# Moving a few small operations at three seams of a fused graph and attention kernel: exponential tables, degrees, the last tile's statistics, and the output bias

## The chip, the cores and the metric

The kernel runs on one core of one Trainium2 chip, as a single program. A core has five engines, each with an instruction stream of its own that it works off in order: TensorE (PE; its weight loads are listed as PEld), VectorE (DVE), ScalarE (ACT), GpSimd (POOL) and SyncE (SP, which here issues all the DMAs). The metric is the device time of one execution in microseconds (us). Where a text here gives a point in time, it is counted from the first instruction of the profiled execution.

## The reference

A graph of 1250 nodes and 41250 edges (each edge in both directions, and a loop at every node), with 512 features per node, goes through four blocks. Each adds its result to `x`, and each starts from a layer normalisation of `x`:

```python
x = x + gnn0(layernorm(x))   # h@wc + (sum over neighbours of h@wn)/count + bias
x = x + ffn0(layernorm(x))   # layernorm; causal attention, 8 heads of 64, q and k l2-normalised;
                             # then 8 experts with gelu, weighted by a softmax gate
x = x + gnn1(layernorm(x))   # layernorm(h@W_self.T + mean_of_neighbours@W_neigh.T + bias)*gamma + beta
x = x + ffn1(layernorm(x))   # depthwise convolution of width 3 over the nodes, added to its input;
                             # qkv; attention over the 16 largest logits per query and head; @wo_w.T + wo_b
```

All of it is in float32. The degree by which `gnn1` divides is the number of edges that end in a node, at least 1.

## The kernel before

The 1250 nodes are cut into T = 10 tiles of P = 125. `X[125, 10, 512]` stays in SBUF through the whole kernel and takes each block's result. The 512 features are K = 4 slices of 128. Products in float32 alternate between a weight load and a matmul on TensorE. What has to be exact runs in a faster format as a high and a low part (the names `hi` and `lo`), with the same matmul done for both.

In nearly all of the kernel the order of instructions is written out by hand (`manual_schedule`); the framework only adds the semaphores. In the experts after the first one and in the first half of the second graph block, the framework's own scheduler chooses the order. What an engine is given later waits behind everything given to it before, also where that waits for another engine.

**Projections to the first attention.** For each tile, q, k and v are made (`project0`), squared and summed (`squares0`, L963 to L967), and the square root is taken on ScalarE (L1054 for q, L1059 for k). q is scaled (L972), turned and kept (`keep_q0`, L977); v is copied to `V` (L1065); k is turned and split into two parts by `keep_k0` (ScalarE L983, then VectorE L984, twice per tile). In the last tile the scores of the first step, `scores0(0, 0)` (TensorE L1034 and L1038), are issued ahead of v. After the loop come the maximum (`largest0`, VectorE L1091), the exponential (`weights0`, ScalarE L1101) and `keep_k0` of the last tile, then three VectorE operations on `deg`: a sum into `edges` (L1212), a maximum with 1 (L1213) and a reciprocal (L1214). `edges` is read at the very end of the kernel and `deg` in the second graph block (`joined1`, L1413).

The first attention has 40 steps (10 tiles by 4 pairs of heads), each for two heads. A step does the scores of the next step, the exponentials, the turns of the step before (`turns0`: TensorE L1122, copies by ScalarE L1127 or VectorE L1125) and the values of the one before that. The two heads' score buffers are one each in PSUM, so the next scores of a head wait until its exponentials have been read. `halves0` makes the split queries for three steps on (ScalarE L1004, GpSimd L1005, two DMAs each).

**Second graph block to the second attention.** In the second graph block each tile is summed over neighbours (L870), joined (L1413), normalised and scaled (L1421, L1422, then GpSimd L1423 and L1424, which writes `X`). The next block starts at once: `stats1` (L636 to L640) and `normed1` (L644) normalise a tile, `turn1_` turns it (TensorE L859, ScalarE L1439 to L1444), and `conv1` does the convolution for a range of tiles and some slices (ScalarE L1453, VectorE L1454 and L1455). `project1_` makes q or k of a range of tiles and some slices (TensorE L1462; q is kept by VectorE L1465, k by ScalarE L1471 and VectorE L1472 twice) and `values1_` makes v (TensorE L1477, VectorE L1483). The three buffers of `ps_mm` go round among all of these products. The output bias `wo_b` is added to `X` by VectorE: for tiles 0 to 7 behind a q or k product of the last tile range (L1530), for tiles 8 and 9 behind the last of them (L1532), and only then is `values1_(6, 7)` issued.

The second attention starts with two DMAs, the split queries of tile 0 (`halves1`: ScalarE L1580, GpSimd L1581, DMAs L1582 and L1583), and the first scores (`scores1`, L1595). Then 40 steps follow, each for two heads: a search for the 16 largest scores (VectorE L1602 to L1626), the exponentials (L1632), a sign that tells the chosen ones (L1639), their product (GpSimd L1642), turns (TensorE L1652, ScalarE L1659) and values (L1708). The values of the last three tiles are made during the first two steps (`values_late1`, `keep_late1` L1747).

ScalarE holds the tables of one set of functions at a time. Where an instruction needs another set, the compiler puts an `ACT_TABLE_LOAD` ahead of it, which the profile lists under that instruction's line.

Of the kernel before, what the change touches and what calls it, by code (L numbers as in the profile page):

```python
# [9 lines left out]
F32 = mybir.dt.float32  # L10
# [5 lines left out]
AF = mybir.ActivationFunctionType  # L16
ALU = mybir.AluOpType
AX = mybir.AxisListType

N = 1250  # L20
P = 125
T = N // P
# [550 lines left out]
def tile_usual(ctx: ExitStack, tc: tile.TileContext, a: dict, out: bass.AP):  # L573
    nc = tc.nc
# [11 lines left out]
    const_pool, const = pool("const", 1, "left")  # L586
# [38 lines left out]
    X = keep.tile([P, T, D], F32, name="X")  # L625
# [3 lines left out]
    deg = keep.tile([P, T], F32, name="deg")  # L629
    edges = keep.tile([P, 1], F32, name="edges")  # L630
# [59 lines left out]
    make_identity(nc, ident)  # L690
    ident16 = const.tile([128, 128], F16, name="ident16")
    nc.gpsimd.tensor_copy(ident16, ident)
    ones = const.tile([P, 1], F32, name="ones")
    nc.gpsimd.memset(ones, 1.0)

# [43 lines left out]
    with (  # L739
# [83 lines left out]
        for r in range(rounds):  # L823
# [7 lines left out]
            while order and (order[0][0] <= r or r == rounds - 1):  # L831
                _, i, t = order.pop(0)
# [10 lines left out]
    def ps_mm():  # L843
        return psum.tile([128, 512], F32, tag="mm", name="ps_mm")
# [28 lines left out]
    w_k = load_w(a["Wk"], "w_k")  # L873
# [82 lines left out]
    def project0(t, w):  # L956
        ps = ps_mm()
        product(ps[:P], hTs[t], 0, w)
        return ps
# [16 lines left out]
    def keep_q0(t, xn):  # L976
        nc.vector.tensor_scalar(qT[:, :, span(t, t + 1)], transposed(xn.rearrange("p h d -> p (h d)")),  # L977
                                qn_g, None, op0=ALU.mult)
# [65 lines left out]
    for t in range(T):  # L1044
        q = project0(t, w_q)
        if turned_k is not None:
            keep_k0(t - 1, turned_k)
        if t == T - 1:
            for n in range(3):
                halves0(n)  # L1050
        norm0(t + 2)
        q_ss = squares0(q)
        turn0(t + 1)
        nc.scalar.sqrt(q_ss, q_ss)  # L1054
        k = project0(t, w_k)
        qn = scaled0(q, q_ss)
        again0(t + 2)
        k_ss = squares0(k)
        nc.scalar.sqrt(k_ss, k_ss)  # L1059
        keep_q0(t, qn)  # L1060
        if t == T - 1:
            scores0(0, 0)
        v = project0(t, w_v)
        kn = scaled0(k, k_ss)
        nc.scalar.copy(V[:, t, :], v[:P])  # L1065
        turned_k = transposed(kn.rearrange("p h d -> p (h d)"))
        hTs.pop(t)
# [17 lines left out]
    with tc.tile_pool(name="att0", bufs=2, side="right", reuse_waits="tile") as at0:  # L1085
# [122 lines left out]
        weights0(0, 0)  # L1208
        keep_k0(T - 1, turned_k)


        nc.vector.tensor_reduce(edges, deg, AX.X, ALU.add)  # L1212
        nc.vector.tensor_scalar(deg, deg, 1.0, None, op0=ALU.max)  # L1213
        nc.vector.reciprocal(deg, deg)  # L1214
        psum_pool.__exit__(None, None, None)
        (ps_t0_pool, ps_t0), (ps_o0_pool, ps_o0), (ps_s0b_pool, ps_s0[1]) = (
            (p, p.__enter__()) for p in (tc.tile_pool(name=name, bufs=1, space=PSUM, reuse_waits="tile")
# [4 lines left out]
        for n in range(len(steps) + 2):  # L1222
            finish0()
            turns = turns0(n - 1)
            fills = fills0(n)

            def turn(last=False):
                for f in turns if last else turns[:1]:
                    f()
                del turns[: len(turns) if last else 1]  # L1230
                for f in fills if last else fills[:1]:
                    f()
                del fills[: len(fills) if last else 1]

            if n > 0:
                largest0(n, 0)
            turn()
            values0(n - 2, 0)
            for f in fills[:1] if n > 36 else ():
                fills.pop(0)()  # L1240
            if n > 0:
                weights0(n, 0)
            largest0(n, 1)
            if len(turns) > 2:
                turn()
            values0(n - 2, 1)
            scores0(n + 1, 0)
            weights0(n, 1)
            if len(turns) > 3:
                turn()  # L1250
            for f in fills[:1] if n > 36 else ():
                fills.pop(0)()
            values0(n - 2, 2)
            sums_over0(n)
            scale0(n - 2)
            if len(turns) > 1:
                turn()
            scores0(n + 1, 1)
            if len(turns) > 1:
                turn()  # L1260
            turn(last=True)
            halves0(n + 3)
            project0()
            if n == 2:
                nc.scalar.copy(b2_h, b2)
                nc.vector.tensor_sub(b2.bitcast(F32R), b2, b2_h.bitcast(F32))
                for i in (1, 3):
                    r = slice(i * E, (i + 1) * E)
                    nc.sync.dma_start(b2_h[r, :].bitcast(F32), b2[r, :])
            if n in (8, 16):  # L1270
                experts[n // 8 - 1] = load_expert(n // 8 - 1)
# [17 lines left out]
    wo_b = row(a["wo_b"], "wo_b", pool=rows1)  # L1289
# [98 lines left out]
    w_k, w_v = (wpool.tile([128, K, D], F32, tag="w", name=name) for name in ("w_k1", "w_v1"))  # L1388
# [59 lines left out]
    def conv1(t0, t1, *ks):  # L1448

        for k in ks:  # L1450
            c = xV[:, t0:t1, k * P : (k + 1) * P]
            at = hT[:, t0:t1, k, :]
            nc.scalar.activation(c, at[:, :, 1 : P + 1], AF.Identity, bias=pos_b[:, k : k + 1], scale=pos_m[:, k : k + 1])  # L1453
            nc.vector.scalar_tensor_tensor(c, at[:, :, :P], pos_w[:, k, 0:1], c, op0=ALU.mult, op1=ALU.add)  # L1454
            nc.vector.scalar_tensor_tensor(c, at[:, :, 2:], pos_w[:, k, 2:3], c, op0=ALU.mult, op1=ALU.add)  # L1455

    def project1_(t0, t1, w, *fs):
        n = (t1 - t0) * P
        for f in fs:
            ps = ps_mm()  # L1460
            for k in range(K):
                nc.tensor.matmul(ps[:, :n], w[:, k, f * 128 : (f + 1) * 128], xV[:, t0:t1, k * P : (k + 1) * P],  # L1462
                                 start=(k == 0), stop=(k == K - 1))
            if w is w_q:
                nc.vector.tensor_scalar(qT[:, f, span(t0, t1)], ps[:, :n], qk_b[:, f : f + 1],  # L1465
                                        float(D) ** -0.5, op0=ALU.add, op1=ALU.mult)
                continue
            for i, (own, other) in enumerate(PAIRS):
                hi, lo = (K2[r, 2 * f + i, span(t0, t1)] for r in (own, other))
                b = qk_b[own, K + f : K + f + 1]  # L1470
                nc.scalar.activation(hi, ps[own, :n], AF.Identity, bias=b)  # L1471
                nc.vector.scalar_tensor_tensor(lo, ps[own, :n], b, hi.bitcast(F32),  # L1472
                                               op0=ALU.add, op1=ALU.subtract)
# [36 lines left out]

    project1_(0, 2, w_q, 0, 1)
    turn1_(T - 2)
    conv1(2, 6, 2, 3)
    project1_(0, 2, w_q, 2, 3)
    stats1(T - 1)
    normed1(T - 1)
    project1_(0, 2, w_k, 0)
    turn1_(T - 1)
    project1_(0, 2, w_k, 1, 2, 3)
    values1_(0, 2)  # L1520
    for f in range(K):
        project1_(2, 6, w_q, f)
        conv1(6, 10, f)
    for f in range(K):
        project1_(2, 6, w_k, f)
    values1_(2, 6)
    for w in (w_q, w_k):
        for f in range(K):
            project1_(6, 10, w, f)
            nc.vector.tensor_add(X[:, f + 4 * (w is w_k), :], X[:, f + 4 * (w is w_k), :], wo_b)  # L1530
    for t in range(8, T):
        nc.vector.tensor_add(X[:, t, :], X[:, t, :], wo_b)  # L1532
    values1_(6, 7)
    manual.__exit__(None, None, None)
    close(slots_pool, work_pool, rows1_pool, gate_pool, stacks_pool, wpool_pool, rows_pool)
# [17 lines left out]
    with (  # L1553
# [17 lines left out]
        def halves1(i, a_):  # L1571
            if i >= T:
                return
            if a_ == 0:
                stacks[i] = at1.tile([128, 2, H, P], F32R, name="stacks")
            S = stacks[i]
            own, other = PAIRS[a_]
            hi, lo = S[own, 0, a_::2, :], S[own, 1, a_::2, :]
            q = qT[own, :, span(i, i + 1)]
            nc.scalar.copy(hi, q)  # L1580
            nc.gpsimd.tensor_sub(lo, q, hi.bitcast(F32))  # L1581
            nc.sync.dma_start(S[other, 1, a_::2, :].bitcast(F32), hi.bitcast(F32))  # L1582
            nc.sync.dma_start(S[other, 0, a_::2, :].bitcast(F32), lo.bitcast(F32))  # L1583

        def scores1(n, a_, *chunks):
            if n > last:
                return
            i, j = steps[n]
            h = 2 * j + a_
            if (n, a_) not in score:  # L1590
                score[n, a_] = ps_s1[a_].tile([P, 3 * 512], F32, name="S")
            for c in chunks:
                n0, n1 = PIECES[a_][c]
                for x in range(2):
                    nc.tensor.matmul(score[n, a_][:, n0:n1], stacks[i][:, x, h, :], K2[:, h, n0:n1],  # L1595
                                     start=(x == 0), stop=(x == 1))
# [168 lines left out]
        with tc.manual_schedule():  # L1765
            nc.sync.dma_start(w_v, a["qkv"][:, 2 * D :].rearrange("(k p) f -> p k f", p=128))
            nc.sync.dma_start(v_b, bass.AP(tensor=a["v_b"].tensor, offset=a["v_b"].offset, ap=[[0, P], [1, D]]))
            for a_ in range(2):
                halves1(0, a_)
            scores1(0, 0, 0, 2, 1)  # L1770
            for n in range(len(steps)):

# [63 lines left out]
            n, i = len(steps), T - 1  # L1836
# [103 lines left out]
```

## Time and profile before

| | |
|---|---|
| median of 3 runs | 1506.62 us (1504.06 to 1507.05) |
| the profiled execution | 1506.82 us |
| its span, first to last instruction | 1504.9 us |
| mean granted TensorE clock | 0.99 |
| busy: PE / DVE / ACT / POOL | 95% / 55% / 47% / 23% |
| table loads on ScalarE | 6, of 1.28 us each |
| PE idle for over 4 us | 3 times: 4.63 us before 322.04, 5.10 before 1021.02, 4.16 before 1110.07 |

The profile is of one execution. A busy share is an average over stages with different limits, so what a change is worth is read from the stretch in which it lies. In the timeline a row gives its start, its length, the engine, the line and the operation with its shapes; where the engine was idle before it, brackets give for how long and what ended that.

### The profile page before, as it was taken

How to read it: one execution, taken by the hardware profiler on the slowest of the kernel's cores; microseconds unless marked ns; L12 is line 12 of the kernel's file. 1: busy time of each engine (PE TensorE's matmuls, PEld its weight loads, DVE VectorE, ACT ScalarE, POOL GpSimd, SP SyncE). 2: the span in 40 equal slices, each digit the busy share in tenths (PEclk: the TensorE clock that was granted, in tenths of full speed). 3: DMA queues.
4: the chain of work that ended last, by engine and by line, in shares of the span. 5: the costliest groups of instructions: out<-in, count | busy, mean ns of one | idle time of the engine just before them, and what ended most of it. 6: DMA issues, size and time to landing. Idle time of an engine off the chain costs nothing. (4 is left out here: it accounts for less than half of the span.)

```text
span 1504.9 us, 22522 instructions
## 1 busy us (share of the span) xinstructions
PE 1424.8 (95%) x8127; PEld 936.5 (62%) x8127; DVE 830.4 (55%) x2852; ACT 707.8 (47%) x1351; POOL 350.1 (23%) x301
## 2 busy tenths in 40 slices
PE   6999999978999998999999999998988999999997
PEld 4566744457778776544544445664447788888885
DVE  8995667644444332341111263565377888887774
ACT  2334434455555553301111122432148999999984
POOL 0110000011111111000000021320026666666662
PEclk9999999989999999999999999999999999999999
DMA  4001000010101000201000000000020001001000
GB/s 141 30 0 57 1 0 1 1 47 16 43 15 49 21 24 18 63 28 56 29 28 28 28 29 29 0 29 0 5 79 15 15 22 25 22 23 25 22 9 24
DMA packets 42332, 41.19 MB, mean 27 GB/s; under 512 B 25738, under 2 KB 30084, under 8 KB 42211
## 3 DMA queue, kind: packets, MB, share of 16 engines
q1 hardware_dynamic: 42211, 39.66, 9.0%
q8 instruction: 66, 1.08, 0.3%
q14 instruction: 55, 0.45, 0.1%
HBM read 26.81 MB, written 2.56 MB: 20 GB/s over the span
## 5 line engine op out<-in xcount | busy, mean ns | idle before, releaser
L1642 POOL TENSOR_TENSOR e<-e,sg 125x1250 f32<-125x1250 f32 x79 | 203.5, 2575 | 127.0 <-ACT sg L1639 75.0
L1602 DVE MAX8 largest<-S 125x8 f32<-125x89 f32 (+1 forms) x1120 | 183.9, 241 | 51.3 <-PE S L1595 51.2
L1336 DVE SCALAR_TENSOR_TENSOR X<-ps_o,gate,X 125x512 f32<-125x512 f32 x80 | 60.0, 749 | 177.1 <-PE ps_o L1334 177.1
L1595 PE MATMUL S<-K,stacks 128*125 128x512 f32 x480 | 133.5, 389 | 14.3 <-ACT sg L1639 6.2
L1334 PE MATMUL ps_o<-we,hid 128*125 128x512 f32 x320 | 141.2, 595 | 0.0
L1659 ACT ACTIVATE pT<-ps_t 125x500 f32<-125x500 f32 x200 | 117.8, 589 | 37.7 <-PE ps_t L1652 32.7
L1652 PE MATMUL ps_t<-ident,e 125*125 125x125 f32 x800 | 132.2, 285 | 2.8 <-ACT pT L1659 1.3
L1652 PEld LDWEIGHTS ps_t<-ident,e 125*125 125x125 f32 x800 | 109.5, 187 | 35.1 <-ACT pT L1659 14.3
L1329 ACT ACTIVATE hid<-ps_mm,b 128x500 f32<-128x500 f32 (+1 forms) x40 | 24.6, 615 | 209.0 <-PE ps_mm L1326 209.0
L1326 PE MATMUL ps_mm<-yT,we 128*128 128x500 f32 (+1 forms) x320 | 115.8, 520 | 0.0
L1708 PE MATMUL O<-pT,yT 125*64 125x125 f32 x1600 | 104.7, 275 | 0.2 <-ACT pT L1659 0.2
L1632 ACT ACTIVATE e<-S,nm 125x1250 f32<-125x1250 f32 x80 | 104.4, 1305 | 0.2
L1639 ACT ACTIVATE sg<-S,below 125x1250 f16<-125x1250 f32 x80 | 104.5, 1307 | 0.0
L1334 PEld LDWEIGHTS ps_o<-we,hid 128*125 128x125 f32 x320 | 59.0, 187 | 72.4 <-issue 69.6
L1127 ACT COPY pT<-ps_t 125x500 f32<-125x500 f32 (+3 forms) x112 | 54.8, 489 | 94.3 <-PE ps_t L1122 93.3
L1326 PEld LDWEIGHTS ps_mm<-yT,we 128*128 128x128 f32 x320 | 60.3, 189 | 55.2 <-issue 53.3
L1595 PEld LDWEIGHTS S<-K,stacks 128*125 128x125 f32 x480 | 72.7, 190 | 33.8 <-ACT sg L1639 18.0
L1708 PEld LDWEIGHTS O<-pT,yT 125*64 125x64 f32 x1600 | 85.8, 136 | 10.5 <-DVE bad L1762 0.8
L1034 PE MATMUL S<-K,stacks 128*125 128x512 f32 (+10 forms) x288 | 84.3, 401 | 7.1 <-ACT e L1101 6.6
L1122 PE MATMUL ps_t<-ident,e 125*125 125x125 f32 x440 | 81.7, 296 | 9.5 <-ACT pT L1127 6.0
L640 ACT ACTIVATE rs<-rs 125x1 f32<-125x1 f32 x60 | 12.1, 203 | 162.9 <-DVE rs L639 159.5
L1005 POOL TENSOR_TENSOR stacks<-yT,stacks 64x125 fp32r<-64x125 f32 x80 | 34.3, 428 | 232.1 <-ACT stacks L1004 229.0
(241 smaller groups left out, 2534.6 us busy)
## 6 DMA issues: line engine op xcount, KB each, us to landing
we<-in_W SPq DMA_DIRECT2D x16, 512.0 KB
stacks<-stacks SPq DMA_DIRECT2D x160, 31.2 KB
stacks<-stacks SPq DMA_DIRECT2D x40, 125.0 KB
X<-in_x SPq DMA_DIRECT2D x5, 500.0 KB
out<-y SPq DMA_DIRECT2D x10, 250.0 KB
w_n<-in_wn SPq DMA_DIRECT2D x1, 1024.0 KB
w_c<-in_wc SPq DMA_DIRECT2D x1, 1024.0 KB
w_q<-in_Wq SPq DMA_DIRECT2D x1, 1024.0 KB
```

The lines of the kernel that those rows point to most:

```text
L1034: nc.tensor.matmul(ps[:, n0:w], stacks[n][:, x, a_, :], K2[:, 2 * j + a_, n0:w], start=(x == 0), stop=(x == 1))
L1122: nc.tensor.transpose(ps[:P, span(t - t0, t - t0 + 1)], es[n, a_][:, span(t, t + 1)], ident[:P, :P])
L1326: nc.tensor.matmul(ps[:, :n], w1[:, k, f * 128 : (f + 1) * 128], yT[:, k, span(t0, t1)], start=(k == 0), stop=(k == K - 1))
L1334: nc.tensor.matmul(ps[:P], hid[:, f, span(t, t + 1)], w2[:, f, :], start=(f == 0), stop=(f == FF // 128 - 1))
L1595: nc.tensor.matmul(score[n, a_][:, n0:n1], stacks[i][:, x, h, :], K2[:, h, n0:n1], start=(x == 0), stop=(x == 1))
L1602: nc.vector.max(out=largest[n, a_][:, k, :], in_=score[n, a_][:, k:N:SEARCHED])
L1632: nc.scalar.activation(e, score[n, a_][:, :N], AF.Exp, bias=maxima.pop((n, a_)))
L1639: nc.scalar.activation(sg, score.pop((n, a_))[:, :N], AF.Sign, bias=belows.pop((n, a_)), accum_out=signs[:, 2 * n + a_ : 2 * n + a_ + 1])
L1642: (nc.vector if 2 * n + a_ == 2 * last + 1 else nc.gpsimd).tensor_mul(e, e, sg)
L1652: nc.tensor.transpose(turned[n, g][:P, span(b - g0, b - g0 + 1)], es[n, b // T][:, span(b % T, b % T + 1)], ident[:P, :P])
L1659: nc.scalar.activation(pTs[n][:, g0:g1, :], turned.pop((n, g))[:P, : (g1 - g0) * P].rearrange("p (t n) -> p t n", n=P), AF.Relu)
L1708: nc.tensor.matmul(outs[n][a_ * DH : (a_ + 1) * DH, :P], V[:, t, h * DH : (h + 1) * DH], pT[:, a_ * T + t, :], start=(t == 0), stop=(t == ...
```

## The change

It makes four edits, at three places.

1. Tables. A one-column tile `spare` is added. ScalarE computes an exponential of `ones` into it twice: in the last tile of the projections, behind the square root for k (L1059), and at the start of the second attention, behind the split queries of tile 0. Nothing reads `spare`.
2. Degrees. The three operations on `deg` go from between `keep_k0` of the last tile and the attention loop to the end of step n = 4 of that loop.
3. Last graph tile. `stats1` and `normed1` of tile 9 and its `turn1_` go ahead of `conv1(2, 6, 2, 3)`, and the four key products of tiles 0 and 1 are issued two before that turn and two behind the convolution, instead of one and three.
4. Output bias. The additions for tiles 8 and 9 go into the key products of tiles 2 to 5, and those for tiles 0 to 7 come ahead of their product's instructions instead of behind them.

```diff
     ident16 = const.tile([128, 128], F16, name="ident16")
     nc.gpsimd.tensor_copy(ident16, ident)
+    spare = const.tile([P, 1], F32, name="spare")
     ones = const.tile([P, 1], F32, name="ones")
     nc.gpsimd.memset(ones, 1.0)
...
         k_ss = squares0(k)
         nc.scalar.sqrt(k_ss, k_ss)
+        if t == T - 1:
+            nc.scalar.activation(spare, ones, AF.Exp)
         keep_q0(t, qn)
...
         weights0(0, 0)
         keep_k0(T - 1, turned_k)
-
-
-        nc.vector.tensor_reduce(edges, deg, AX.X, ALU.add)
-        nc.vector.tensor_scalar(deg, deg, 1.0, None, op0=ALU.max)
-        nc.vector.reciprocal(deg, deg)
...
             halves0(n + 3)
             project0()
+            if n == 4:
+
+                nc.vector.tensor_reduce(edges, deg, AX.X, ALU.add)
+                nc.vector.tensor_scalar(deg, deg, 1.0, None, op0=ALU.max)
+                nc.vector.reciprocal(deg, deg)
...
     project1_(0, 2, w_q, 0, 1)
     turn1_(T - 2)
-    conv1(2, 6, 2, 3)
     project1_(0, 2, w_q, 2, 3)
     stats1(T - 1)
     normed1(T - 1)
-    project1_(0, 2, w_k, 0)
+    project1_(0, 2, w_k, 0, 1)
     turn1_(T - 1)
-    project1_(0, 2, w_k, 1, 2, 3)
+    conv1(2, 6, 2, 3)
+    project1_(0, 2, w_k, 2, 3)
     values1_(0, 2)
     for f in range(K):
         project1_(2, 6, w_q, f)
         conv1(6, 10, f)
     for f in range(K):
+        if f < T - 8:
+            nc.vector.tensor_add(X[:, 8 + f, :], X[:, 8 + f, :], wo_b)
         project1_(2, 6, w_k, f)
     values1_(2, 6)
     for w in (w_q, w_k):
         for f in range(K):
+            t = f + 4 * (w is w_k)
+            nc.vector.tensor_add(X[:, t, :], X[:, t, :], wo_b)
             project1_(6, 10, w, f)
-            nc.vector.tensor_add(X[:, f + 4 * (w is w_k), :], X[:, f + 4 * (w is w_k), :], wo_b)
-    for t in range(8, T):
-        nc.vector.tensor_add(X[:, t, :], X[:, t, :], wo_b)
     values1_(6, 7)
...
             for a_ in range(2):
                 halves1(0, a_)
+            nc.scalar.activation(spare, ones, AF.Exp)
             scores1(0, 0, 0, 2, 1)
```

## The prediction

> **What bounds the kernel now.** I read the page first, then the timeline around the lines of the diff, then the windows view for the granted clock.
>
> ```profile
> PE 1424.8 (95%) x8127; PEld 936.5 (62%) x8127; DVE 830.4 (55%) x2852; ACT 707.8 (47%) x1351; POOL 350.1 (23%) x301
> ```
>
> PE is busy 95%, so the stages themselves are PE's; what an edit off PE can win is a hole in PE. Three holes over 4 us lie where the diff works, and nowhere else is PE idle longer than 1.3 us. I call them A (projections to first attention), B (second graph layer's last tile) and C (projections to second attention).
>
> Timeline, A (start, duration, engine, line; idle before and its releaser in brackets):
>
> ```profile
> 313.00 0.59 ACT L1065 COPY V<-ps_mm 125x512 f32<-125x512 f32 x1 [3.20 <-PE ps_mm L865]
> 313.60 1.28 ACT L1101 ACT_TABLE_LOAD   x1
> 314.90 1.09 ACT L1101 ACTIVATE e<-S,nm 125x1000 f32<-125x1000 f32 x1
> ...
> 318.92 0.16 DVE L1212 TENSOR_REDUCE edges<-deg 125x1 f32<-125x10 f32 x1
> 319.57 1.20 DVE L1091 TENSOR_REDUCE nm<-S 125x1 f32<-125x1000 f32 x1
> 320.80 1.09 ACT L1101 ACTIVATE e<-S,nm 125x1000 f32<-125x1000 f32 x1 [2.68 <-DVE nm L1091]
> ...
> 322.04 1.62 PE L1034 MATMUL S<-K,stacks 128*125 128x512 f32 x3 [4.63 <-ACT e L1101]
> ```
>
> The table load stands in the chain: load, first e, two rounds of keys (ACT L983, DVE L984), degrees, maximum, second e, PE. ACT had been idle 3.20 us just before.
>
> Timeline, B and C:
>
> ```profile
> 1014.17 1.27 POOL L1424 TENSOR_TENSOR X<-X,u 125x512 f32<-125x512 f32 x1
> 1014.27 1.70 DVE L1454 SCALAR_TENSOR_TENSOR yT<-slot,pos_w,yT 128x500 f32<-128x500 f32 x1 [1.66 <-ACT yT L1453]
> 1018.87 0.68 DVE L636 BATCH_NORM_STATS2 st<-X 125x6 f32<-125x512 f32 x1
> 1021.02 1.10 PE L859 MATMUL ps_tp<-ident,h 125*128 125x125 f32 x4 [5.10 <-DVE h L644]
> ...
> 1105.45 1.71 DVE L1530 TENSOR_TENSOR X<-X,wo_b 125x512 f32<-125x512 f32 x1
> 1107.09 2.16 DVE L1532 TENSOR_TENSOR X<-X,wo_b 125x512 f32<-125x512 f32 x2
> 1109.28 0.69 DVE L1483 TENSOR_TENSOR yT<-ps_mm,v_b 125x512 f32<-125x512 f32 x1
> 1110.07 4.56 PE L1595 MATMUL S<-K,stacks 128*125 128x512 f32 x12 [4.16 <-DVE yT L1483]
> 1115.46 1.28 ACT L1632 ACT_TABLE_LOAD   x1 [9.54 <-DVE nm L1612]
> ```
>
> In B the statistics of tile 9 stand behind four convolution operations, though its X was complete at 1015.44. In C the last value eviction stands behind three bias additions, stretched because GpSimd's L1581 runs from 1105.37 to 1108.09.
>
> Windows view (stretch, length, PE busy, PEclk, DMA share, GB/s):
>
> ```profile
> 321.00:331.10 10.10, 8.39 (x25) 0.50 0.06 14
> 600.90:604.20 3.30, 1.96 (x16) 1.00 0.02 5
> 604.30:607.60 3.30, 3.30 (x14) 0.50 0.00 0
> 1106.10:1109.40 3.30, 0.00 (x0) 1.00 0.56 117
> 1109.50:1116.20 6.70, 6.13 (x15) 0.50 0.08 16
> ```
>
> After each hole the granted clock is halved: 10.1 us in A, 6.7 in C, and in B the 3.3 us from 1020.7.
>
> **The change, seam A.** The table load moves into ACT's 3.20 us of idle: 1.28 plus a one-column exponential of about 0.2 (L640 takes 0.203) fit, so e starts right behind V at 313.6: 1.28 saved. If that cover were gone, V would be late by what sticks out. Nothing else is queued on ACT there. A rule to weigh: the Trainium skill (ScalarE: Activation LUTs, "What ACT_TABLE_LOAD costs") puts a switch at 1283 ns of load plus some 1380 ns of drain. The load agrees with the trace's 1.28; the drain does not show, since e starts 0.02 us behind it; with it A would gain another 1.4 (an estimate from that page). The three degree operations take 318.92 to 319.57, 0.65, all on the chain: saved. Second e at 318.87 instead of 320.80: 1.93. The degrees come back at n = 4, on DVE between L1125 and L1091 at 357.07. The maximum there ends near 358.5, and e at 358.62 starts 0.04 behind ACT's own copy, so there is no slack: 0.55 given back (bounds 0 to 0.65). Their reader, L1413, comes 600 us later. Net 1.38.
>
> What is late next: PE does not wait for the first e any more (its 1.22 hole closes), but its hole before the second e is still 316.2 to 320.1, 3.9 us. If the clock still falls, as before, the net stays 1.38. If not, the steps n = 0 and 1 run at full speed. Replayed with the unthrottled durations (scores 0.94 for three instead of 1.62, transposes 0.60 for four instead of 1.04), the e of n = 2 comes 2.1 sooner. So 1.38 to 3.5.
>
> **Seam B.** PE order is now q0, q1, turn 8, q2, q3, k0, k1, turn 9, k2, k3, v0, v1. Statistics start when GpSimd delivers X, 1015.44 instead of 1018.87. With the five small operations as in the trace (1.55 from L636 to L644) h is ready at 1017.6; PE has k0 to 1015.9 and k1 (1.85) to 1017.75, so the 5.10 hole is covered. That wait stands on DVE with only the key evictions behind it: ACT L1471, also behind the square root, resumes at 1017.1. Two key columns of four alternating operations (0.47 each, one overlapping) end at 1020.6, turn 9 copies to 1021.0, two ACT convolutions 1022.5, four DVE ones 1024.8. Only then come k2's evictions: 1026.3. PE has three buffers; v1 needs k2's and so starts at 1026.3, against 1028.06 + 3.43 = 1031.5 before. Gain 5.1. The next stage needs the convolution at 1029.8, five after it is ready. Bounds: 3.4, if only the earlier statistics count, and 6.4, if no eviction holds PE (5.10 plus about 1.3 of slow matmuls).
>
> **Seam C.** The ten bias additions go to places where DVE waits for PE or ACT (0.41 to 2.02 idle before L1465 and L1472; the existing eight already fit there). So L1483 runs at 1106.1, 0.2 behind PE's last matmul, to 1106.8; it reads PSUM and I take it as not slowed by GpSimd, as L1734 keeps 268 to 273 ns in a loop where POOL is two thirds busy. What is late next is a transfer: the transfers' semaphore events put the landing of the second half of the first stack at 1109.05 (issued 1106.64). PE can start at about 1109.1, not 1106.9: 0.97 of 4.16. ACT loads the table at 1105.9 in 9.5 us of idle: 1.28 less before e and sg, hence before PE's next scores at 1119.40. DVE's next search (1120.85) waits only 0.16 for those, so its own chain gains 0.97 + 0.16 while PE and ACT gain 0.97 + 1.28. Between the two, 1.7. With the clock held, the first six matmuls take 1.41 (as at 1119.40) instead of 2.43, and both chains win another 1.1: 2.8. Bounds 1.1 to 3.3.
>
> **Sum.** 1.38 + 5.1 + 1.7 = 8.2, against the profiled execution's 1506.82 (span 1504.9): 1498.6. The median of the three runs is 0.2 lower, so 1498.4. Between the seams PE is at 297.6 of 299 us (627 to 926) and 70.9 of 71 (1035 to 1106), and both attention loops are chains of PE, ACT and DVE, so an earlier start arrives at the end.
>
> **Rivals.** (1) The clock holds in A and C, whose holes shrink to 3.9 and 3.1: another 2.1 + 1.1, 1495.2. For it: holes up to 1.3 at full work left the clock alone. Against it: it fell at 604.3 after a stretch with PE still 1.96 of 3.30 busy, so a hole need not be whole. The Trainium skill (TensorE: Matmul & The Clock Gate, "What's actually happening") lets the clock fall after a whole idle window of about 3.4 us; by that rule C never falls and A seldom, and the row at 604.3 contradicts it. Chance 0.25. (2) The loads do not move: the result `spare` is used by nothing and might be dropped, or a second load be placed before e. Then 1.28 in A and about 0.9 in C are lost: 1500.6, chance 0.08. (3) B gets a wait in place of the one removed: v1 and the next stage behind late evictions, B worth 2 instead of 5.1: 1501.5, chance 0.07. (4) Slower: shifted work meets the clock's windows at a bad place in the second attention loop (1117 to 1480), where PE has holes of 0.9 to 1.1 in several steps. A fall costs 1 to 2.1 as in C and A; six dearest ones (12.6) make it 4.4 slower, 1511, and four break even. Against it: not one fall there before. Chance 0.05.
>
> **How the numbers follow.** The forecast has 0.55. The range goes from rival 1 less 0.7 for B's upper bound, 1494.5, to rival 3 with the degrees' bound, 1502. A measurement here tells about 0.2% (3 us) from no change: faster means under 1503.6. All but rival 4 lie there, less a tail of 0.05 where two of the smaller gains fail together: faster 0.90, same 0.05, slower 0.05.
>
> **What would show it.** A: a table load near 310, behind L1059, and no 1.22 hole; second e 5.3 behind the first instead of 5.9. B: PE without a hole over 1.3 from q0 to v1. C: scores released by a transfer or issue, about 3.2 after the last value matmul; no load before L1632. The PEclk row tells forecast from rival 1. The prediction is wrong if a hole over 4 us is left at a seam, or if the loops' steps (mean 9.1 in the second) get longer.

## The result, and the profile after

The changed kernel takes 1495.57 us (median of 4 runs, 1495.13 to 1496.06) against 1506.14 (4 runs, 1504.06 to 1507.05): a ratio of 0.9932, 95% interval 0.992 to 0.9945. In a second measurement (e12 below) the ratio was 0.993, 0.9918 to 0.9942. A ratio, here and below, can differ a little from the quotient of the two medians beside it, since it is not taken from them. The change is faster by 10.6 us, inside the range on record; the forecast, 1498.4, was 2.8 too high. The profiled execution took 1495.83, with a span of 1493.8.

Lines past the edits have other numbers in the changed kernel (L1101 is now L1104, L1595 is L1600).

Timeline after, seam A:

```profile
309.69 1.28 ACT L1062 ACT_TABLE_LOAD   x1
310.99 0.20 ACT L1062 ACTIVATE spare<-ones 125x1 f32<-125x1 f32 x1
...
312.86 0.59 ACT L1068 COPY V<-ps_mm 125x512 f32<-125x512 f32 x1 [1.67 <-PE ps_mm L866]
313.34 1.10 ACT L1104 ACTIVATE e<-S,nm 125x1000 f32<-125x1000 f32 x1
...
318.61 1.09 ACT L1104 ACTIVATE e<-S,nm 125x1000 f32<-125x1000 f32 x1 [2.04 <-DVE nm L1094]
...
319.85 1.02 PE L1035 MATMUL S<-K,stacks 128*125 128x512 f32 x3 [3.97 <-ACT e L1104]
```

The load lies in ScalarE's idle time, e follows V at once, the second e is 5.27 behind the first (5.90 before), and PE's hole is 3.97.

Timeline after, where the degrees went:

```profile
353.85 0.15 DVE L1265 TENSOR_REDUCE edges<-deg 125x1 f32<-125x10 f32 x1
...
354.37 2.76 DVE L1094 TENSOR_REDUCE nm<-S 125x1 f32<-125x1250 f32 x2
...
355.86 1.30 ACT L1104 ACTIVATE e<-S,nm 125x1250 f32<-125x1250 f32 x1 [0.51 <-DVE nm L1094]
```

ScalarE now waits 0.51 for the maximum behind them, where it did not wait before.

Timeline after, seams B and C:

```profile
1009.67 1.27 POOL L1428 TENSOR_TENSOR X<-X,u 125x512 f32<-125x512 f32 x1
...
1010.97 0.69 DVE L636 BATCH_NORM_STATS2 st<-X 125x6 f32<-125x512 f32 x1 [0.72 <-POOL X L1428]
...
1013.15 0.65 PE L860 MATMUL ps_tp<-ident,h 125*128 125x125 f32 x4
...
1021.89 3.67 PE L1481 MATMUL ps_mm<-w_v,yT 128*125 128x512 f32 x8 [1.29 <-DVE K L1476]
...
1096.41 1.28 ACT L1775 ACT_TABLE_LOAD   x1
1096.42 0.69 DVE L1487 TENSOR_TENSOR yT<-ps_mm,v_b 125x512 f32<-125x512 f32 x1 [0.51 <-PE ps_mm L1481]
...
1099.68 4.57 PE L1600 MATMUL S<-K,stacks 128*125 128x512 f32 x12 [3.31 <-DMA stacks<-stacks]
...
1105.10 1.30 ACT L1637 ACTIVATE e<-S,nm 125x1250 f32<-125x1250 f32 x1 [7.19 <-DVE nm L1617]
```

In B the statistics follow GpSimd's X directly, the turn of tile 9 has no hole before it, and the new wait on a late key eviction is 1.29. In C the value eviction is done at 1097.1, but PE waits for a transfer until 1099.68.

Windows after (stretch, length, PE busy, weight loads, VectorE, ScalarE, GpSimd, PEclk, DMA share, GB/s):

```profile
317.30:320.50 3.20, 0.65 (x3) 0.57 (x4) 1.92 (x4) 1.66 (x4) 0.36 (x2) 1.00 0.00 0
320.70:327.30 6.60, 5.93 (x21) 4.82 (x20) 1.76 (x3) 3.42 (x6) 0.92 (x3) 0.50 0.09 22
1095.50:1098.70 3.20, 0.88 (x3) 0.05 (x1) 1.10 (x2) 2.36 (x4) 2.31 (x2) 1.00 0.27 58
1098.90:1105.60 6.70, 5.92 (x14) 4.29 (x15) 3.28 (x20) 0.50 (x1) 0.00 (x0) 0.50 0.20 44
```

The clock still falls in A and C (from 1.00 to 0.50 in the PEclk column), though PE was busy 0.65 and 0.88 of the 3.2 us before. There is no fall at 1020 any more, and none near 600.

Where the time came from, read off as how much sooner the same instruction starts than in the kernel before, differenced from mark to mark. The marks are: the last sum of squares; the exponentials of n = 2 and n = 5 of the first attention; the first expert product; the first q product of tiles 2 to 5; the end of the last value product ahead of the second attention, and there the exponentials of n = 1. All numbers are us sooner, from one profiled execution of each kernel.

| stretch | after | e12 | e1 | e2 | e3 | e4 | e5 |
|---|---|---|---|---|---|---|---|
| to the last sum of squares | 0.13 | 1.69 | 1.95 | 1.55 | 1.68 | -0.47 | 1.62 |
| A: to n = 2 | 3.10 | 3.08 | 1.23 | 2.47 | 0.54 | 0.33 | 0.06 |
| n = 2 to 5 (degrees) | -0.47 | -0.47 | 0.01 | -0.45 | 0.03 | -0.01 | 0.00 |
| n = 5 to the first expert | 1.70 | 1.65 | 0.16 | 1.56 | 1.54 | 1.55 | 1.52 |
| B: to q of tiles 2 to 5 | 5.07 | 4.98 | -0.23 | -0.23 | 5.02 | -0.60 | -0.72 |
| to the last value product | 0.00 | 0.00 | 0.00 | 0.00 | 0.00 | 0.00 | 0.00 |
| C: to n = 1 | 1.68 | 1.66 | -1.64 | -1.66 | -0.02 | 1.53 | 1.37 |
| to the end | -0.15 | 0.01 | 0.00 | 0.10 | 0.09 | 0.08 | -0.06 |
| span sooner | 11.06 | 12.60 | 1.48 | 3.34 | 8.88 | 2.41 | 3.79 |

Two rows are chance. In the first, no edit lies ahead: 1.5 to 2.0 us is there whenever the clock did not fall near 20 us, as it did in the kernel before. In the fourth, 1.5 us is there whenever it did not fall near 604, and e3, e4 and e5, which change nothing between its two marks, have that too. So 1.5 of the 11.06 belongs to the one execution profiled before, not to the change. How far a row varies by itself shows where its edit is missing: -0.23 to -0.72 in row B, and 0.06 to 0.54 in row A (e3, e4, e5).

### The profile page after: what moved, and what is told of

Same layout as the page of the kernel before. It is cut to its first block, busy times and chain, and to the rows that moved or that the text cites. A ratio compares the mean times of both kernels' runs of the same rounds, so it can differ in the third digit from the quotient of the medians.

```text
span 1493.8 us, 22522 instructions
## 1 busy us (share of the span) xinstructions
PE 1420.2 (95%) x8127; PEld 933.3 (62%) x8127; DVE 826.1 (55%) x2852; ACT 708.1 (47%) x1353; POOL 349.9 (23%) x301
## 3 DMA queue, kind: packets, MB, share of 16 engines
q8 instruction: 66, 1.08, 0.3%
## 5 line engine op out<-in xcount | busy, mean ns | idle before, releaser
L1600 PE MATMUL S<-K,stacks 128*125 128x512 f32 x480 | 133.8, 389 | 13.1 <-ACT sg L1644 5.8
L1600 PEld LDWEIGHTS S<-K,stacks 128*125 128x125 f32 x480 | 72.9, 191 | 32.2 <-ACT sg L1644 17.1
```

## The experiments

The first five are the kernel before with one part of the change each.

**e1, the table at A alone.**

```diff
...
         nc.scalar.sqrt(k_ss, k_ss)
+        if t == T - 1:
+            nc.scalar.activation(spare, ones, AF.Exp)
```

> The kernel before with one edit: the exponential into `spare` behind the last tile's square root (seam A). Chain theory: the table load leaves the chain, the first and the second exponential of the attention come 1.28 us sooner, PE's hole before the second scores shrinks from 4.63 to 4.6 at most (its first part closes), and the gain arrives at the end: 1.3 us sooner. If the low clock behind the hole gets shorter by a window, another 1.2. Rival (the load is hidden anyway, the keys behind it set the pace): under 0.3. Rival (a drain of 1.4 us goes with a load, as the Trainium skill has it): the first exponential 2.7 sooner.

Measured: 1505.24 against 1505.83, ratio 0.9988 (0.9978 to 0.9999). The first exponential comes 1.43 us sooner, counted from the last sum of squares, and 1.23 are left at n = 2 with a low clock of 10.2 us as before. So the load was on the chain. 1.43 is the load and some 0.15 of overlap with the copy of V; a drain of 1.4 behind it would have made it 2.7 and is not seen. Further on, this execution lost 1.64 at C, where the clock was low in two pieces, from 1106.5 and from 1116.7, instead of one. e2 has the same there, and neither edit is near.

**e2, the degrees alone**: the three operations taken from ahead of the loop and put at the end of step n = 4.

```diff
...
+            if n == 4:
+                nc.vector.tensor_reduce(edges, deg, AX.X, ALU.add)
...
```

> The kernel before with one edit: the three degree operations at the end of step n = 4. Chain theory: the second exponential comes 0.65 us sooner, the exponentials of n = 5 have given 0.5 of it back, so 0.1 to 0.2 is left at the end. Rival (VectorE has slack at n = 4): all 0.65 is kept.

Measured: 1506.47 against 1505.83, ratio 0.9999 (0.9988 to 1.0009). From the first exponential of the attention to the second 0.64 is gained, and from n = 4 to n = 5 0.48 is lost: the chain theory, to 0.1. The 1.8 more at n = 2 comes with a low clock of 6.8 us instead of 10.2 at a hole of 3.98.

**e3, the statistics of B alone.**

```diff
-    conv1(2, 6, 2, 3)
     project1_(0, 2, w_q, 2, 3)
     stats1(T - 1)
     normed1(T - 1)
-    project1_(0, 2, w_k, 0)
+    project1_(0, 2, w_k, 0, 1)
     turn1_(T - 1)
-    project1_(0, 2, w_k, 1, 2, 3)
+    conv1(2, 6, 2, 3)
+    project1_(0, 2, w_k, 2, 3)
```

> The kernel before with one edit: the last tile's statistics, turn and two key products ahead of the convolution (seam B). Chain theory: PE's first product of tiles 2 to 5 comes 5.0 us sooner, with one new wait of 0.7 to 1.3 us before the second value product, no low clock at 1020, and all 5.0 arrive at the end. Rival (the late convolution and evictions hold the next stage): about 2. The low clocks at 321, 604 and 1109 stay as before.

Measured: 1499.38 against 1505.83, ratio 0.9957 (0.994 to 0.9974). B gives 5.02, all of it still there at the second attention; the new wait is 1.28 and the low clock at 1020 is gone. This edit alone is most of the change. The two clocks that were expected to stay did not quite: 604 is absent, and the one in A was low for 13.7 us.

**e4, the bias of C alone.**

```diff
...
+            t = f + 4 * (w is w_k)
+            nc.vector.tensor_add(X[:, t, :], X[:, t, :], wo_b)
             project1_(6, 10, w, f)
-            nc.vector.tensor_add(X[:, f + 4 * (w is w_k), :], X[:, f + 4 * (w is w_k), :], wo_b)
-    for t in range(8, T):
-        nc.vector.tensor_add(X[:, t, :], X[:, t, :], wo_b)
...
```

> The kernel before with one edit: the output bias ahead of the evictions (seam C). Theory (a transfer becomes the bound): the first scores start 0.9 us sooner, released by the second transfer of the first split queries, not 3 us sooner; the load of the table stays in the chain; about 1.0 us at the end. Rival (the bias additions were the whole hole): the first scores start some 0.3 behind the last value eviction, 3 us sooner, and the end comes 3 sooner.

Measured: 1503.8 against 1505.78, ratio 0.9985 (0.9973 to 0.9996). The first scores start 0.85 sooner, with a hole of 3.31 left: the transfer had taken the additions' place. At n = 1 it is 1.53; the rest goes with a low clock of 3.4 instead of 6.8 us.

**e5, the table at C alone.**

```diff
...
                 halves1(0, a_)
+            nc.scalar.activation(spare, ones, AF.Exp)
```

> The kernel before with one edit: the exponential into `spare` behind the split queries of tile 0 (seam C). Chain theory: the first exponential there comes 1.28 us sooner; VectorE's second pair of searches, which waited only 0.16 for PE, gains 0.16, and what arrives at the end lies between 0.16 and 1.28, about 0.7. Rival (load hidden anyway): 0.

Measured: 1503.71 against 1505.78, ratio 0.9986 (0.9974 to 0.9997). The first scores start where they did, the first exponential 1.36 sooner, and 1.37 is left at n = 1 and 1.31 at the end: nothing is lost to VectorE's searches. Counted from the last value product, the third search comes only 0.33 sooner, but the fourth, which in the kernel before waited 0.33 for PE, comes 1.35 sooner. So the exponentials of n = 1 hang on the chain from the sign to PE's scores, value product and turn, and not on the searches.

Windows of e5, the place of the fall near 604:

```profile
599.20:602.40 3.20, 1.91 (x15) 1.27 (x13) 1.81 (x6) 1.49 (x7) 0.09 (x1) 1.00 0.02 5
602.60:605.80 3.20, 3.20 (x22) 2.37 (x23) 0.29 (x1) 0.43 (x2) 0.01 (x1) 1.00 0.00 0
```

With the same code and PE as busy (1.91 of 3.20, before 1.96 of 3.30), the clock stays up here.

The next ones change the changed kernel. Their ratios are to the kernel before; the points in time are compared with the changed kernel.

**e6, PE kept busy in the hole of A.**

```diff
             scores0(n + 1, 0)
+            if n == 0:
+                fill = ps_o0.tile([128, 512], F32, tag="o", name="O")
+                for k in range(4):
+                    nc.tensor.matmul(fill[:P], w_v[:, k, :P], w_v[:, k, :], start=(k == 0), stop=(k == 3))
             weights0(n, 1)
```

> The changed kernel with four products whose result nothing reads, in PE's hole before the second scores of seam A. Clock theory: PE has no hole over 1 us there, the clock does not fall at 320, and the exponentials of n = 2 come 1 to 2 us sooner; as much at the end. Rival (ScalarE and VectorE set the pace there, whatever the clock): 0, or later by what the products stick out.

Measured: 1495.49 against 1505.78 for the kernel before, ratio 0.9918 (0.9891 to 0.9945), not to be told from the changed kernel. The timeline and the windows of e6 (columns as above):

```profile
317.37 5.37 PE L1250 MATMUL O<-w_v 128*125 128x512 f32 x8 [1.61 <-DVE K L985]
```

```profile
314.30:317.50 3.20, 1.59 (x9) 1.02 (x8) 1.72 (x3) 1.34 (x4) 0.00 (x0) 1.00 0.71 266
317.70:320.90 3.20, 3.20 (x5) 1.19 (x4) 1.95 (x3) 1.66 (x4) 0.81 (x3) 0.50 0.00 0
```

The products' PSUM buffer is one that the last keys still read, so they began behind 1.61 us of idle; the clock fell behind a stretch in which PE was busy 1.59 of 3.20, and the products, at half speed, stuck out: the next scores came 2.4 later and n = 2 0.6 later. The experiment was badly sized and tells nothing on the clock's price; e11 repeats it with two products.

**e7, PE kept busy in the hole of C.**

```diff
     values1_(6, 7)
+    fill = ps_sm()
+    for k in range(3):
+        nc.tensor.matmul(fill[:P], w_v[:, k, :P], w_v[:, k, :], start=(k == 0), stop=(k == 2))
```

> The changed kernel with three products whose result nothing reads, in PE's hole of 3.31 us at seam C. Clock theory: the first scores start at the same point (the transfer), the first six matmuls take 1.4 us instead of 2.4, and the second attention's steps and the end come about 1.1 sooner. Rival: VectorE's searches set the pace there, whatever the clock: under 0.3.

Measured: 1493.85 against 1505.78, ratio 0.9919 (0.989 to 0.9948). The clock does not fall at C. The first scores start at the same distance from the last value product, the first exponential comes 1.08 and that of n = 1 1.53 sooner, and 1.5 stay to the end. So the low clock costs C 1.5, with the transfer as it is.

**e8, the first split queries early.**

```diff
+    first_stack = qkv1.tile([128, 2, H, P], F32R, name="stacks")
+    for own, other in PAIRS:
...
+        nc.sync.dma_start(first_stack[other, 1, a_::2, :].bitcast(F32), hi.bitcast(F32))
+        nc.sync.dma_start(first_stack[other, 0, a_::2, :].bitcast(F32), lo.bitcast(F32))
     values1_(2, 6)
...
-            for a_ in range(2):
-                halves1(0, a_)
+            stacks[0] = first_stack
             nc.scalar.activation(spare, ones, AF.Exp)
```

> The changed kernel with the split queries of tile 0 made and sent before the last range's products (into a tile of their own) instead of at the start of the second attention. Transfer theory: the first scores are then released by the last value eviction, 0.3 to 0.8 us behind PE's last value product instead of 3.31, the clock does not fall at seam C, and the end comes 2.5 + 1.1, about 3.5, sooner. Rival (another wait, the last keys or the release of PSUM, stands right behind the transfer): under 1.5.

Measured: 1493.78 against 1506.12, ratio 0.9919 (0.9901 to 0.9937). The timeline of e8:

```profile
309.21 0.20 ACT L1062 ACTIVATE spare<-ones 125x1 f32<-125x1 f32 x1
309.44 0.20 ACT L1783 ACTIVATE spare<-ones 125x1 f32<-125x1 f32 x1
...
1095.55 2.54 PE L1609 MATMUL S<-K,stacks 128*125 128x512 f32 x12 [0.83 <-issue]
...
1099.87 1.28 ACT L1646 ACT_TABLE_LOAD   x1 [6.41 <-DVE nm L1626]
```

The first scores start 2.48 sooner, 0.83 behind the last value product: the transfer was the bound. But of the 3.5 put on record only 1.08 is left at n = 1. With no split queries ahead of it in its block, the second exponential into `spare` hung on nothing and was given out at 309, behind the first one, so the load came back into the chain; PE then waited 2.29 us for the first sign, and the clock fell at 1104.3. The rival that the table loads do not move has happened here, by the order of the program.

**e9, the degrees in VectorE's waiting time.**

```diff
             sums_over0(n)
+            if n == 4:
+                nc.vector.tensor_reduce(edges, deg, AX.X, ALU.add)
...
             scale0(n - 2)
```

> The changed kernel with the degree operations behind the reciprocal of the sums of step n = 4, where VectorE waits for the next copy, instead of at the end of that step. Theory: the 0.5 us that the exponentials of n = 5 lost come back, 0.5 sooner at the end. Rival (that loss came from elsewhere): 0.

Measured: 1493.39 against 1506.12, ratio 0.9916 (0.9895 to 0.9936). From n = 2 to n = 5 the loss of 0.47 is gone (0.48 sooner than the changed kernel): the place decides, not the operations. The further difference is in two stretches without an edit: 1.65 ahead of A, where the clock did not fall near 20 us, and 0.46 at C, where it was low for 3.4 us instead of 6.8.

**e10, all three together**: the edits of e6, e8 and e9.

```diff
...
+    first_stack = qkv1.tile([128, 2, H, P], F32R, name="stacks")
...
+                for k in range(4):
...
             sums_over0(n)
+            if n == 4:
...
```

> The changed kernel with the early split queries, the degrees in VectorE's waiting time, and the filling products in the hole of seam A. If the parts add up: 3.5 + 0.5 + 1 to 2, so 5 to 6 us sooner than the changed kernel, about 1490. Rival (the holes close but the loops absorb an earlier start): under 2.

Measured: 1492.86 against 1506.12, ratio 0.9913 (0.9897 to 0.993). That is 2.7 below the changed kernel and not the 5 to 6 put on record. The profiled execution, at 1490.09, is the fastest of four; the others took 1492.81 to 1493.34 at a mean granted clock of 0.996 instead of 0.999. In its profile the clock falls nowhere between the first instructions and the end: 1.10 sooner at n = 2, 0.49 by the degrees, 2.74 at C with the load still in the chain. The parts add up as far as the clock stays up.

**e11, the same with the load held back, and e12, the changed kernel again.** The edit of e11, against e10:

```diff
...
+    nc.scalar.activation(spare, ones, AF.Exp)
     values1_(6, 7)
     manual.__exit__(None, None, None)
...
-            nc.scalar.activation(spare, ones, AF.Exp)
             scores1(0, 0, 0, 2, 1)
...
-                for k in range(4):
+                for k in range(2):
```

> As e10, but the second exponential into `spare` stands behind the last keys on ScalarE (in e8 and e10 it had been given out right behind the first one, near 309, so that the load came back into the chain), and two filling products instead of four. Theory: no table load before the first exponential of the second attention, which comes 2.5 + 1.1 sooner than in the changed kernel, counted from PE's last value product; the fillers fit into the hole, with no low clock at 320 and the exponentials of n = 2 of the first attention 1 to 1.8 sooner. In all 5 to 6 us under the changed kernel, about 1490. Rival (PE's next wait, for the signs, eats the load's gain): 1.3 less, about 1491.5.

> The changed kernel once more, beside e11 on one chip: 1495 to 1496, a ratio of 0.993 to the kernel before, and a second profile that shows whether the low clock at 604 stays away: if that was luck, it may be there; if the earlier start keeps it away, it isn't.

Measured on one chip: e11 1488.43 (1487.56 to 1489.44), ratio to the kernel before 0.9885 (0.9871 to 0.99); e12 1494.94, ratio 0.993 (0.9918 to 0.9942). e11 beats both kernels, the changed one by 6.5 us, and the intervals do not touch. The timeline of e11:

```profile
1091.17 1.28 ACT L1550 ACT_TABLE_LOAD   x1
...
1093.23 2.54 PE L1613 MATMUL S<-K,stacks 128*125 128x512 f32 x12 [0.83 <-ACT spare L1550]
...
1097.58 1.30 ACT L1650 ACTIVATE e<-S,nm 125x1250 f32<-125x1250 f32 x1 [4.91 <-DVE nm L1630]
```

Against the changed kernel it gains 2.14 at A, 0.50 at the degrees and 4.01 at C. In the profiled execution the clock does not fall at any seam; two of the four took 1489.2 to 1489.4 at a mean granted clock of 0.997 instead of 0.999, so there it fell somewhere. e12 repeats the table of the changed kernel in every row but the first and the last, the fall near 604 absent again.

## Why the prediction was right, and where its sum was off

**Seam A.** The steps held: the load in idle time (1.43 for 1.28), the degrees (0.64 for 0.65), the hole of 3.97 for 3.9, and 0.49 of 0.55 given back at n = 4. Mis-sized was the term for the clock: I let the low clock cost what it had cost before, and it lasted 6.8 us instead of 10.2, so A gave 3.10 at n = 2 and not 1.93. It did the same in e7, e8, e9 and e12, and in e2 with the degrees alone, all with holes of 3.97 to 3.99; behind holes of 4.6 (before, e1, e4, e5) it was 10.2. In e3, with a hole of 3.86, it was 13.7, but there the clock fell at 314.7, 1.8 us ahead of the hole, so the length does not follow from the hole alone.

The traces do show what it follows. Within one execution all falls lie whole multiples of 3.413 us apart: those of the kernel before, at 20.6, 321.0, 604.3, 1020.7 and 1109.4, are steps 0, 88, 171, 293 and 319. Over the 14 profiled executions, ahead of the low clock at the program's end, the clock stayed low after each of the 24 low steps in which PE was busy for 2.78 us or less, and rose after each of the 35 in which it was busy for 2.87 or more. At A, before (three steps) and after (two):

```profile
321.00:324.40 3.40, 2.36 (x7) 1.91 (x8) 1.35 (x3) 1.46 (x4) 1.19 (x3) 0.50 0.07 17
324.40:327.80 3.40, 2.73 (x10) 2.05 (x10) 1.11 (x1) 2.55 (x5) 0.00 (x0) 0.50 0.08 21
327.80:331.20 3.40, 3.40 (x13) 2.66 (x12) 0.17 (x1) 1.94 (x5) 0.55 (x2) 0.50 0.02 5
...
320.60:324.00 3.40, 2.73 (x11) 2.20 (x9) 1.69 (x2) 1.61 (x3) 0.73 (x2) 0.50 0.17 43
324.00:327.40 3.40, 3.39 (x11) 2.75 (x11) 0.17 (x1) 1.90 (x6) 0.30 (x1) 0.50 0.00 0
```

Before, the first step still holds the end of the hole and the second another gap; after, PE is busy in all of the second step, and the clock is back.

**Seam B.** Right in size (5.07 and 4.98 for 5.1) and in mechanism: statistics at X, the covered hole, the wait for k2's eviction before v1. That wait was 1.29, at the upper end of the 0.7 to 1.3 put on record for e3.

**Seam C.** 1.68 for 1.7, but by two errors that cancel. The transfer as the next bound was right (a hole of 3.31 for 3.2; 0.85 of 4.16, for 0.97). The step that VectorE's chain gains only 0.16 from the load was wrong: that is about so for its next search (0.33 in e5), but the one after that waits for PE, and e5 keeps 1.37 of the load. And the low clock, which I had taken as it was, costs more once the load is gone: the value product ahead of PE's second scores ran at half speed until 1105.6 and took 4.40 (3.60 in e5), and the scores right behind it took 1.72 instead of 1.41. e7, without the low clock, gains 1.53 where I had put 1.1.

**The sum.** 8.2 was forecast and the spans differ by 11.06: 1.2 more in A (1.0 of it by the clock), 1.5 from a fall near 604 in the execution profiled before, which was no part of the change, and small rests. The medians differ by 10.6. They are of executions with other falls, of which no trace is kept; on record is that longer runs of the kernel before have the lower mean clock (0.987 at 1509.58, 0.991 at 1503.9, in the measurement of e1). The loops kept their steps: 9.20 us in the mean in the second attention, before and after.

**Rivals.** Rival 1 named 1495.2, and 1495.57 was measured, but that is luck, and its mechanism is refuted: the clock fell in A and C. Its prices were too low besides: without the fall e11 gains 2.14 in A on top of the 1.0 above, where 2.1 stood for both, and e7 gains 1.53 in C, where 1.1 stood. Its rule from the Trainium skill (TensorE: Matmul & The Clock Gate, "What's actually happening"), a whole idle window, is not what these runs show: falls came with PE busy 0.65, 0.88, 1.59 and 1.96 us of the 3.2 to 3.3 before. Rival 2 did not come true in the changed kernel and did in e8. Rivals 3 and 4 did not: B lost nothing behind its new wait, and no fall lies in the loop of the second attention beyond its first steps.

What stays open is when the clock falls. From 15 us on, it fell after every full-speed step with PE busy for 1.54 us or less of 3.41 (32 of 32) and after none with more than 2.08, but between 1.55 and 2.08 it fell after 5 of 28, and the traces do not settle which: the step near 600 had 2.07 in the kernel before and in e1, which fell, and 2.08 in e5, which did not. With the four products of e6 the step in A had 1.80 and the clock fell; it stayed up in e10 at 1.80 and in e11 at 1.95. So what e10 and e11 gain in A by the clock rests in part on luck. One fall more or less moved an execution by 1.5 to 2.0 us in the first and fourth rows of the table.

## What to carry to other kernels

At a seam, list everything that must be there before the bottleneck engine can start, with its time, before pricing the removal of the latest: in C three additions were worth 0.85 us of a hole of 4.16 because a transfer stood right behind them, and sending that transfer earlier was worth 2.5 more. An operation moved "to later" is only hidden where its engine waits at that point: the same 0.65 us cost 0.48 in one place of a step and nothing in another. A dummy instruction that is to load a table must stand in the order behind something of its own engine; with nothing ahead of it, in e8, it was given out 786 us ahead of the scores that it stood by in the program (309.44 against 1095.55), and the load came back.

## What the runs showed of the hardware that I had not expected

- The granted clock can halve without an idle stretch: after a step of 3.41 us with PE busy for 1.80 of it in e6 and for 2.07 in the kernel before. It is then low for one to four such steps (3.4 to 13.7 us), until PE has been busy for 2.87 or more of one.
- A table load costs 1.28 us, and nothing more shows beside it: the next exponential began 0.02 behind it. Moving it gained 1.43 in A, with some 0.15 by overlap with the copy of V, and 1.36 in C.
- The four transfers of the first split queries, of 125 KB each and issued 0.6 to 1.3 us apart, each landed 2.4 to 2.5 us behind their issue, by the trace's semaphore events.
- A VectorE addition of two SBUF operands that took 0.69 alone took 1.71 beside GpSimd's subtraction (1105.45 in the kernel before), while the value eviction, which reads PSUM, kept 0.69 beside it (1096.42 in the changed kernel).
